# A two-layer convolution-attention hybrid on one Trainium2 core: the order of the first loads, the place of the feed-forward weights, and the first table load

## The chip, the cores and the metric

The kernel runs on one core of a Trainium2 chip. The metric is the device time of one execution in microseconds (us); lower is better. The engines are TensorE (PE, with its weight loads shown apart as PEld), VectorE (DVE), ScalarE (ACT), GpSimd (POOL) and SyncE (SP), which only issues DMAs here. ScalarE and GpSimd can issue DMAs too.

## What is computed

The input x has 4 images of 128 channels and 64 x 64 positions, so each image is a 128 x 4096 matrix. Cut to what matters:

```python
# layer 0, for each image (C = 128 channels, 4096 positions)
xn = group_norm(x)                                  # 32 groups of 4 channels
e1, e2 = prelu(w1 @ xn + b1), prelu(w2 @ xn + b2)   # 64 channels each
asm = prelu(wa @ xn + ba)                           # 128 channels
x = x + softmax(e1.T @ e2, axis=2) @ asm            # 4096 x 4096 scores
# layer 1, on tokens t = x.T (4096 tokens of 128 features)
h = layer_norm(t)
q = products_of_cosines(h + rx_theta)               # 16 heads of 8
a = softmax(q @ q.T / sqrt(8)) @ q                  # q is query, key and value
x1 = layer_norm(h + a @ w_comb.T + b_comb) * g1 + beta1
zf = cos(x1[..., :8]) * cos(ry_theta)
t = t + layer_norm(x1 + relu(zf @ w1.T + b1) @ w2.T + b2) * g2 + beta2
# a recurrence over the positions, y = sigmoid(norm(W t) + y @ V.T)
t = t + recurrence(layer_norm(t))
```

Attention runs per image over all 4096 tokens in layer 1.

## The kernel before

The images are taken one after the other. For each, `first_stage` runs layer 0 (and, beside it, the feed-forward of the image before), and `second_stage` runs layer 1's attention. `last_stage` does the last image's feed-forward, and the recurrence over all images ends the kernel. The order of instructions on TensorE, ScalarE and VectorE is written out by hand within the stages; each engine works its list in order. DMAs and SyncE's list are placed by a scheduler, which also inserts the waits, among them the waits for memory: each stage has pools of tiles, a new stage's tiles lie where earlier tiles lay, and an instruction that writes such a tile waits for the last user of what lay there.

**The start** (lines 135 to 331). GpSimd's queue issues the loads of the first convolutions' weights and biases (`w12_sb`, `b12_sb`, `wa_sb`, `aa_sb`, `a12_sb`), then clears small tiles and builds the group matrix `grp` with two `affine_select`. ScalarE's queue issues 26 loads (line 184 on): `rx_bc`, `wc_sb`, two copies of four bias rows into `biases`, the feed-forward's matrices and rows, and four copies each of `f1T` and `ry`. SyncE issues x in four pieces of 128 x 1024 (`load_x`, line 1513), the third and fourth only when the first and second have landed.

VectorE, once x arrives, takes eight statistics (`gst`, line 350), and between them small preparations: it negates slopes and biases (lines 167 to 169), and turns the bias rows `ba`, `b_comb` and `fb2 + be1` into pairs of a rounded part and a rest in `bias_rows` (lines 324 to 330). `gmv` (line 353), two tiny matmuls with `grp` (lines 357 and 366) and GpSimd's power (line 241) give the mean `gm` and the scale `r_g`. Then come the feed-forward's first weights (lines 312 to 322): `cos_steps` brings `ry` into range on VectorE and ScalarE takes its sine (`cry`), `f1_all` is multiplied by it, split into `f1_sb` and `f1_low`, and a DMA from SyncE puts part of `f1_low` into `f1_sb`. The tiles of this preparation lie in a pool `setup`, closed at line 331; the image's tile `q` may lie on that memory afterwards.

**Layer 0** (`layer0`, line 369). `normalised` writes the normalised image into `q` (line 378), the convolutions follow (lines 391 and 427), `halves` splits e1 into a high and a low part (`hl`), and the loop at line 545 runs over 8 blocks of 512 positions with 32 tiles of scores each, two pairs of tiles a turn: `scores` (line 503, then `exp` at line 507), `weigh` (line 514, with the row sums on VectorE at lines 525 and 528). After each pair the loop calls `meanwhile`, which advances other work by a step: `calls[0]` counts these calls, 16 in a block. From the 18th call, `tokens` (line 606) does a finished block's transposition, sums, layer norm, cosines (table switch and sine at line 255) and products, and stores high and low parts in `parts_dram` (line 699).

**Attention** (`attention`, line 701) loads `queries` and `keys` from `parts_dram` (lines 762 and 771), has GpSimd clear and fill `q_aug` and `mirror` (lines 731 to 748 and 802), and then works through score tiles: line 1057 (scores), 1069 (exponential), 866 and 845 (the two products), 832 (transposition on VectorE).

Of the kernel before, what the change touches and what calls it, by code (L numbers as in the profile page):

```python
# [26 lines left out]
def kernel(  # L27
# [109 lines left out]
    def load(ap, name, shape=None):  # L137
        t = const.tile(list(shape or ap.shape), F32, tag=name, name=name)
        loader[0].dma_start(out=t, in_=ap)
        return t  # L140

    def load_row(ap, name):
        return load(ap.partition_broadcast(P), name, (P, ap.shape[-1]))
# [29 lines left out]
    for sign, base in ((1, 0), (-1, 3)):  # L173
# [7 lines left out]
            channel_multiplier=sign,  # L181
        )
    grp = grp.rearrange("p a b -> p (a b)")
    loader[0] = nc.scalar
    rx_bc = load_row(rx, "rx_bc")
    wc_sb = load(w_combT, "wc_sb")

    f1_sb = const.tile([P, NF, P], F32, tag="f1_sb", name="f1_sb")
    ry_sb = once.tile([P, 1], F32, tag="ry_sb", name="ry_sb")
    nc.gpsimd.memset(ry_sb, 0.0)  # L190
    setup = ctx.enter_context(ExitStack())
    setup_pool = setup.enter_context(tc.tile_pool(name="setup", bufs=1, reuse_waits="tile"))
    f1_all, f1_low = (
        setup_pool.tile([P, NF * P], F32, tag=name, name=name) for name in ("f1_all", "f1_low")
    )
    biases = setup_pool.tile([33, 4, P], F32, tag="biases", name="biases")
    nc.gpsimd.memset(f1_all, 0.0)
    for i in range(2):
        for k, ap in enumerate((ba, b_comb, fb2, be1)):
            nc.scalar.dma_start(out=biases[ds(32 * i, 1), k, :], in_=ap)  # L200
    for g in range(4):
        nc.scalar.dma_start(out=f1_all[ds(D * g, D), :], in_=f1T)
        nc.scalar.dma_start(out=ry_sb[ds(D * g, D), :], in_=ry)
    fb1_sb, f2_sb = load(fb1, "fb1_sb"), load(f2T, "f2_sb")
    g1_bc, be1_z = load_row(g1, "g1_bc"), const.tile([P, D], F32, tag="be1_z", name="be1_z")
    be1_bc = setup_pool.tile([P, P], F32, tag="be1_bc", name="be1_bc")
    nc.scalar.dma_start(out=be1_bc, in_=be1.partition_broadcast(P))
    g2_bc, be2_bc = load_row(g2, "g2_bc"), load_row(be2, "be2_bc")
    WT_sb, VT_sb = load(WT, "WT_sb"), load(VT, "VT_sb")
    gamma_sb, beta_sb = load(gamma, "gamma_sb"), load(beta, "beta_sb")  # L210


    nc.vector.tensor_copy(be1_z, be1_bc[:, 0:D])
    ident = const.tile([P, P], F32, tag="ident", name="ident")
    make_identity(nc, ident)
    ones = const.tile([P, P], F32, tag="ones", name="ones")
# [27 lines left out]
    def cos_steps(dst, arg, k, r):  # L244

        nc.vector.tensor_scalar(k, arg, 1.0 / (2 * math.pi), ROUND, ALU.mult, ALU.add)
        nc.vector.tensor_scalar(k, k, ROUND, None, ALU.subtract)
        nc.vector.scalar_tensor_tensor(r, k, -TWO_PI_1, arg, ALU.mult, ALU.add)
        yield
        nc.vector.scalar_tensor_tensor(r, k, -TWO_PI_2, r, ALU.mult, ALU.add)  # L250
        nc.vector.scalar_tensor_tensor(r, k, -TWO_PI_3, r, ALU.mult, ALU.add)
        yield
        nc.vector.scalar_tensor_tensor(r, r, -1.0, r, ALU.mult, ALU.max)
        yield
        nc.scalar.activation(dst, r, AF.Sin, bias=half_pi[: dst.shape[0]], scale=-1.0)
# [53 lines left out]
        return bc.unsqueeze(1).broadcast_to([P, TG, P])  # L309


    ck = once.tile([P, 1], F32, tag="ck", name="ck")
    cr = once.tile([P, 1], F32, tag="cr", name="cr")
    cry = once.tile([P, 1], F32, tag="cry", name="cry")
    for _ in cos_steps(cry, ry_sb, ck, cr):
        pass
    nc.vector.tensor_scalar(f1_all, f1_all, cry, None, ALU.mult)
    f1_high = f1_sb.rearrange("p f e -> p (f e)")
    nc.vector.tensor_copy(f1_high.bitcast(F32R), f1_all)
    nc.vector.tensor_tensor(f1_low, f1_all, f1_high, ALU.subtract)  # L320

    nc.sync.dma_start(out=f1_high[ds(2 * D, 2 * D), :], in_=f1_low[ds(2 * D, 2 * D), :])

    for row in (0, 32):
        at = slice(row, row + 1)
        nc.vector.tensor_tensor(biases[at, 2], biases[at, 2], biases[at, 3], ALU.add)
        nc.vector.tensor_copy(bias_rows[at].bitcast(F32R), biases[at, 0:3])
    nc.vector.tensor_tensor(
        bias_rows[at].bitcast(F32R), biases[at, 0:3], bias_rows[at], ALU.subtract
    )  # L330
    setup.close()


    def prelu(dst, src, plus, minus, bias, minus_slope):

# [1238 lines left out]
    def first_stage(im, before):  # L1574


        n = im["n"]


        ffn = dict(x1=(HALF, 3), fhalf=(HALF, 7), hT=(MID, 2))  # L1580
        held_late = dict(thalf=(HALF, 6), half=(HALF, 2), hl=(MID, 2))
        rest = dict(e=(BIG, 2), big=(BIG, 1), mid=(MID, 7), sums=(MID, 2))
        pools = {**ffn, **held_late, **rest}
        psum = dict(ps_acc=(ONE, 1), ps_pair=(MID, 2), ps_one=(ONE, 3))
        engines = {nc.tensor.engine, nc.scalar.engine, nc.vector.engine}
        others = {name: one_psum for name in ("ps_norm", "ps_tok")}
        with stage(f"conv{n}", {}, others, **pools, **psum), tc.manual_schedule(engines=engines):
            own, calls = [], [0]
            step_late = in_steps(feed_forwards(before) if before else [], 13, 3)

            def meanwhile(steps=1):

                calls[0] += 1
                if before and calls[0] in (14, 17, 20):
                    before["left"].pop(0)()
                for _ in range(steps):
                    step_first(own)

                for _ in range(0 if calls[0] <= 8 else 2 if calls[0] % 8 == 0 else 1):
                    step_late()  # L1600

            norm = im["norm"] or list(norm_stats(n, im["xs"]))[-1]
            layer0(
                n,
                im["xs"],
                im["q"],
                norm,
                n == "r",
                lambda ic, sums: own.append(tokens(im, ic, sums)),
                meanwhile,  # L1610
            )
            *own, tail = own
            for g in own:
                for _ in g:
                    pass
            while step_late():
                pass
            while not next(tail):
                pass
        return tail  # L1620
# [119 lines left out]
    t2_rows = [t2_dram[ts(n, P), :] for n in range(N)]  # L1740
    before = None
    x_next = {"xs": load_x(0, ts(0, P))}

    def prepare_image(n):

# [5 lines left out]

    for n in range(N):
        image = open_image(n, ts(n, P), "right" if n % 2 else "left", **x_next)
        tail = first_stage(image, before)
        if before:
            before["close"]()
        upcoming = prepare_image(n + 1) if n + 1 < N else iter(())
        second_stage(image, tail, upcoming)
        before = image
# [246 lines left out]
```

## Time and profile before

| what | us |
|---|---|
| median of 3 runs | 6988.64 |
| lowest and highest | 6988.06, 6990.65 |
| profiled execution, device time | 6989.88 |
| its span, first to last instruction | 6988.2 |
| mean granted TensorE clock in it | 0.989 |
| image 0, first normalisation starts | 24.34 |
| image 0, one block of layer 0 | 44.0 |
| image 0, first attention scores | 405.1 |

The profile is of one execution. Its page gives each engine's busy time over the span, and the views used below list instructions in order of time. A line of such a list has the start, the duration, the engine, the source line, the operation with what it writes and reads, and in brackets how long the engine had been idle and which work ended the idle time. "SPq" and "ACTq" are an engine's sequencer issuing a DMA; the bytes travel afterwards. Buffer numbers are left out of names, so `f_sb` is `f1_sb`, `minus_b` is `minus_b12`, `s` and `p` are any of the score and exponential tiles.

### The profile page before, as it was taken

The page shows a single profiled execution, that of the slowest core. Times are in us where ns is not written, and L with a number is a line of the kernel's source. Part 1 is how long each engine was busy: PE and PEld are TensorE (multiplying, and loading weights), DVE is VectorE, ACT ScalarE, POOL GpSimd, SP SyncE. Part 2 cuts the span into 40 slices and gives each one's busy share as a digit, 9 for nine tenths or more (in the row PEclk, how much of TensorE's full clock was granted, in tenths as well). Part 3 has the DMA queues.
Part 4 walks back from the last instruction along what each step waited for, and adds up shares of the span by engine and source line. Part 5 has one row for each costly group of instructions (what it writes and reads, how often), then busy time and mean ns, then how long its engine had stood idle before and what let it go on. Part 6 is the DMA issues. An engine that isn't in the chain of part 4 may idle for free. (4 is left out here: it accounts for less than half of the span.)

```text
span 6988.2 us, 223483 instructions
## 1 busy us (share of the span) xinstructions
PE 6812.8 (97%) x92333; PEld 3660.6 (52%) x92333; DVE 5967.8 (85%) x8064; ACT 5932.7 (85%) x11843; POOL 2786.7 (40%) x10008
## 2 busy tenths in 40 slices
PE   8999999999999999999999999999999999999996
PEld 4545555555664555555565455555466555555554
DVE  6688889987888999888787888888978888898987
ACT  4479999996669999999566999999956699999984
POOL 1134444434333444443433344444343434344442
PEclk9999999999999999999999999999999999999998
DMA  1110000000111000000111100000001100000012
GB/s 32 37 41 25 24 28 21 22 10 23 49 50 42 26 21 22 21 22 9 33 50 49 37 22 21 22 20 24 22 26 47 56 25 22 22 24 29 13 62 109
DMA packets 84760, 219.87 MB, mean 31 GB/s; under 512 B 9384, under 2 KB 10288, under 8 KB 82960
## 3 DMA queue, kind: packets, MB, share of 16 engines
q1 hardware_dynamic: 80448, 200.34, 8.4%
q8 instruction: 726, 11.89, 0.7%
q10 hardware_dynamic: 3024, 4.99, 0.2%
q14 instruction: 306, 2.51, 0.1%
q0 software_dynamic: 256, 0.13, 0.0%
HBM read 141.44 MB, written 56.62 MB: 28 GB/s over the span
## 5 line engine op out<-in xcount | busy, mean ns | idle before, releaser
L1069 ACT ACTIVATE e<-s 128x1024 f32<-128x1024 f32 (+1 forms) x3480 | 2950.0, 901 | 114.8 <-PE s L1057 83.0
L832 DVE STREAM_TRANSPOSE t<-e 128x1024 f32<-128x1024 f32 x2240 | 2594.2, 1210 | 77.3 <-ACT e L1069 74.6
L845 PEld LDWEIGHTS misc<-t,mirror 128*32 128x32 f32 x57344 | 1656.6, 110 | 1327.2 <-issue 1270.8
L845 PE MATMUL misc<-t,mirror 128*32 128x128 f32 x57344 | 1968.3, 273 | 18.6 <-DVE later L859 15.8
L1069 ACT ACTIVATE xs<-s 128x1024 f32<-128x1024 f32 (+1 forms) x2152 | 1838.9, 908 | 55.2 <-PE s L1057 43.0
L832 DVE STREAM_TRANSPOSE t<-xs 128x1024 f32<-128x1024 f32 x1344 | 1562.5, 1210 | 42.7 <-ACT xs L1069 41.2
L866 PE MATMUL acc<-e,q_aug 128*32 128x512 f32 x11360 | 1524.7, 609 | 1.0 <-POOL q_aug L748 1.0
L1057 PE MATMUL s<-queries,keys 32*128 32x512 f32 x9216 | 1243.2, 497 | 20.7 <-ACT e L1069 10.4
L912 POOL COPY own<-o 32x36 f32<-32x36 f32 x2048 | 430.7, 210 | 1807.1 <-DVE o L904 1727.1
L514 PE MATMUL acc<-p,asmT 128*128 128x512 f32 x2048 | 946.2, 593 | 1.8 <-DVE e L410 1.6
L866 PE MATMUL acc<-xs,q_aug 128*32 128x512 f32 x7072 | 942.4, 605 | 0.0
L507 ACT ACTIVATE p<-s 128x1024 f32<-128x1024 f32 x512 | 499.8, 1022 | 403.8 <-PE s L503 399.8
L1057 PEld LDWEIGHTS s<-queries,keys 32*128 32x128 f32 x9216 | 487.2, 182 | 601.4 <-issue 296.2
L937 POOL COPY other<-turned 32x64 f32<-32x64 f32 x1904 | 449.7, 236 | 624.3 <-DVE turned L927 545.8
L1069 ACT ACTIVATION_READ_ACCUMULATOR e<-s 128x1 f32 x2880 | 694.5, 241 | 0.0
L802 POOL COPY mirror<-q 32x128 f32<-32x128 f32 x2048 | 599.3, 293 | 199.2 <-PE misc L845 111.3
L503 PE MATMUL s<-hl,e 128*128 128x512 f32 x2048 | 586.4, 428 | 22.4 <-ACT p L507 10.9
L528 DVE TENSOR_TENSOR total<-total,p 128x1024 f32<-128x1024 f32 x448 | 547.8, 1223 | 22.0 <-ACT p L507 14.3
L514 PEld LDWEIGHTS acc<-p,asmT 128*128 128x128 f32 x2048 | 380.0, 190 | 334.8 <-issue 309.8
L503 PEld LDWEIGHTS s<-hl,e 128*128 128x128 f32 x2048 | 379.9, 189 | 178.3 <-issue 68.6
L1069 ACT ACTIVATION_READ_ACCUMULATOR xs<-s 128x1 f32 x1728 | 421.4, 244 | 0.0
L898 POOL COPY by_token<-by_key 32x4 f32<-32x4 f32 x2000 | 383.8, 192 | 84.4
(314 smaller groups left out, 4459.2 us busy)
## 6 DMA issues: line engine op xcount, KB each, us to landing
keys<-parts_dram SPq DMA_DIRECT2D x256, 256.0 KB
queries<-parts_dram SPq DMA_DIRECT2D x1024, 32.0 KB
x_dram<-x SPq DMA_DIRECT2D x56, 256.0 KB
fx<-x_dram SPq DMA_DIRECT2D x48, 256.0 KB
xs<-in_x_dram SPq DMA_DIRECT2D x16, 512.0 KB
t_dram<-t2T SPq DMA_DIRECT2D x32, 256.0 KB
t2s<-t_dram SPq DMA_DIRECT2D x16, 512.0 KB
hl<-hl SPq DMA_DIRECT2D x28, 256.0 KB
```

Source lines behind the costliest of these rows:

```text
L503: nc.tensor.matmul(s[:, j, :], stationary, moving, start=y == 0, stop=y == len(parts) - 1)
L507: nc.scalar.activation(p, s, AF.Exp)
L514: nc.tensor.matmul(state["acc", ic], asmT[:, ts(2 * jp + j, P)], p[:, j, :], start=jp == 0 and j == 0, stop=jp == NP - 1 and j == 1,)
L528: nc.vector.tensor_tensor(state[ic], state[ic], p, ALU.add)
L802: nc.gpsimd.tensor_copy(wv[ts(a, 32), s, :, :, ts(a, D)], own[ts(s, 32)])
L832: nc.vector.transpose(group["e"][h][:, k, :], es[h])
L845: nc.tensor.matmul(state["acc"][ts(2 * x + h, 32), :], state["w"][:, QT * (s // 4) + TG * x + s % 4, h, :], state["e"][h][:, :, ds(IC * x ...
L866: nc.tensor.matmul(it["in"]["acc"][ts(2 * h + x, 32), :], it["qa"][:, ds((2 * it["tiles"][x] + h) * V, 32)], it["e"][h][:, ts(x, IC)], sta ...
L912: nc.gpsimd.tensor_copy(own[ts(s, 32), ts(x, 4), h, :], ov[ts(2 * h + x, 32), s, :, 0:V])
L937: copy(to[ts(k, 32), h], tv[ts(2 * x + h, 32), k])
L1057: nc.tensor.matmul(ss[h][:, x, :], keys[unit[x] // QT].bitcast(F32R)[r, ts(unit[x] % QT, P)], queries[b].bitcast(F32R)[r, :], start=True, ...
L1069: nc.scalar.activation(es[h][:, ts(x, IC)] if split else es[h], ss[h][:, x, :] if split else ss[h].rearrange("p x c -> p (x c)"), AF.Exp, ...
```

## The change

The loads of x are issued first, by SyncE. Behind them SyncE issues the loads that ScalarE's queue issued before. Of the bias rows only `ba`, which layer 0 needs, is prepared at the start, by a new function `bias_of_third` that borrows the last columns of `q` as room. The rest of the preparation becomes a generator `other_weights`, which takes its room from the pool of feed-forward tiles (`fhalf`, unused in image 0) and is advanced in the calls 6, 26, 29 and 32 of `meanwhile` in image 0. A one-column exponential at the start makes ScalarE load exp's table. The pool `setup` is gone, and so the addresses of other tiles change.

The removed lines at the start, in short, are the loads on ScalarE's queue and the preparation named above (old lines 184 to 213 and 312 to 331). The added ones:

```diff
+    def bias_of_third(room):
+        for row in (0, 32):
+            nc.scalar.dma_start(out=room[row : row + 1, :], in_=ba)
+        for row in (0, 32):
+            at = slice(row, row + 1)
+            nc.vector.tensor_copy(bias_rows[at, 0].bitcast(F32R), room[at, :])
+        nc.vector.tensor_tensor(
+            bias_rows[at, 0].bitcast(F32R), room[at, :], bias_rows[at, 0], ALU.subtract
+        )
+
+    def other_weights():
+        f1_all, f1_low, rows, row = (
+            get("fhalf", name) for name in ("f1_all", "f1_low", "bias_parts", "be1_row")
+        )
+        biases = rows[0:33].rearrange("p (k e) -> p k e", e=P)
+        be1_bc = row[:, 0:P]
+        nc.gpsimd.memset(f1_all, 0.0)
+        nc.gpsimd.memset(ry_sb, 0.0)
+        for i in range(2):
+            for k, ap in enumerate((b_comb, fb2, be1)):
+                nc.sync.dma_start(out=biases[ds(32 * i, 1), k, :], in_=ap)
+        for g in range(4):
+            nc.sync.dma_start(out=f1_all[ds(D * g, D), :], in_=f1T)
+            nc.sync.dma_start(out=ry_sb[ds(D * g, D), :], in_=ry)
+        nc.sync.dma_start(out=be1_bc, in_=be1.partition_broadcast(P))
+        yield
+        nc.vector.tensor_copy(be1_z, be1_bc[:, 0:D])
+        cr, cry = (once.tile([P, 1], F32, tag=name, name=name) for name in ("cr", "cry"))
+        for _ in cos_steps(cry, ry_sb, ck, cr):
+            pass
+        yield
+        nc.vector.tensor_scalar(f1_all, f1_all, cry, None, ALU.mult)
+        f1_high = f1_sb.rearrange("p f e -> p (f e)")
+        nc.vector.tensor_copy(f1_high.bitcast(F32R), f1_all)
+        nc.vector.tensor_tensor(f1_low, f1_all, f1_high, ALU.subtract)
+        yield
+        nc.sync.dma_start(out=f1_high[ds(2 * D, 2 * D), :], in_=f1_low[ds(2 * D, 2 * D), :])
+        for row in (0, 32):
+            at = slice(row, row + 1)
+            nc.vector.tensor_tensor(biases[at, 1], biases[at, 1], biases[at, 2], ALU.add)
+            nc.vector.tensor_copy(bias_rows[at, 1:3].bitcast(F32R), biases[at, 0:2])
+        nc.vector.tensor_tensor(
+            bias_rows[at, 1:3].bitcast(F32R), biases[at, 0:2], bias_rows[at, 1:3], ALU.subtract
+        )
...
-            own, calls = [], [0]
+            own, calls, weights = [], [0], other_weights()
...
                 calls[0] += 1
+                if n == 0 and calls[0] in (6, 26, 29, 32):
+                    next(weights, None)
...
     x_next = {"xs": load_x(0, ts(0, P))}
+    loader[0] = nc.sync
+    rx_bc = load_row(rx, "rx_bc")
+    wc_sb = load(w_combT, "wc_sb")
+    f1_sb = const.tile([P, NF, P], F32, tag="f1_sb", name="f1_sb")
+    ry_sb, ck = (once.tile([P, 1], F32, tag=name, name=name) for name in ("ry_sb", "ck"))
+    be1_z = const.tile([P, D], F32, tag="be1_z", name="be1_z")
+    fb1_sb, f2_sb = load(fb1, "fb1_sb"), load(f2T, "f2_sb")
+    g1_bc, g2_bc, be2_bc = load_row(g1, "g1_bc"), load_row(g2, "g2_bc"), load_row(be2, "be2_bc")
+    WT_sb, VT_sb = load(WT, "WT_sb"), load(VT, "VT_sb")
+    gamma_sb, beta_sb = load(gamma, "gamma_sb"), load(beta, "beta_sb")
...
         image = open_image(n, ts(n, P), "right" if n % 2 else "left", **x_next)
+        if n == 0:
+            bias_of_third(image["q"][:, S - P : S])
+            nc.scalar.activation(ck, half_pi, AF.Exp)
         tail = first_stage(image, before)
```

In layer 0's list on ScalarE this puts a sine table load, the sine `cry` and an exp table load between the exponentials of score tiles 9 and 10 of block 1 (blocks and tiles counted from 0).

More of the change, by code (lines that the diff above doesn't have):

```diff
@@ L183 @@
     grp = grp.rearrange("p a b -> p (a b)")
[L184 to L213, printed above, removed]
     ident = const.tile([P, P], F32, tag="ident", name="ident")
@@ L309, in row4 @@
         return bc.unsqueeze(1).broadcast_to([P, TG, P])
[L312 to L331, printed above, removed]
+    def bias_of_third(room):
[7 more added lines that the diff above has]
+        )
```

## The prediction

> **What bounds the kernel now.** I read the page first, then busy time by stretch, then the first 45 us in order of time, then the place where layer 0 hands over to attention.
>
> ```profile
> span 6988.2 us, 223483 instructions
> PE 6812.8 (97%) x92333; PEld 3660.6 (52%) x92333; DVE 5967.8 (85%) x8064; ACT 5932.7 (85%) x11843; POOL 2786.7 (40%) x10008
> ```
>
> TensorE is busy 97% of the span, so work saved on another engine counts only where TensorE stands still for it. Busy time by stretch (columns: stretch, length, busy time and instructions of PE, PEld, DVE, ACT and POOL, granted clock, DMA share, GB/s) shows where that is:
>
> ```profile
> 0.00:25.00 25.00, 1.20 (x5) 1.05 (x5) 11.80 (x37) 1.58 (x2) 7.78 (x21) 1.00 0.37 122
> 110.00:154.00 44.00, 44.00 (x150) 25.40 (x149) 30.83 (x53) 20.66 (x22) 5.53 (x8) 1.00 0.10 30
> 405.00:450.00 45.00, 37.56 (x488) 16.05 (x486) 43.54 (x64) 39.95 (x83) 25.08 (x75) 0.89 0.07 21
> ```
>
> In the first 25 us TensorE does almost nothing. One block of layer 0 lasts 44 us, all of it TensorE's, while VectorE has 13.2 us and ScalarE 23.3 us to spare. In the first 45 us of attention VectorE is the full engine (43.54 of 45). The change touches all three. The start, in order of time (start, duration, engine, line, operation; in brackets the idle time before and its releaser):
>
> ```profile
> 5.69 0.69 DVE L350 BATCH_NORM_STATS2 gst<-xs 128x6 f32<-128x512 f32 x1 [4.41 <-DMA xs<-in_x_dram]
> ...
> 8.40 0.15 DVE L169 TENSOR_SCALAR minus_b<-b_sb 128x1 f32<-128x1 f32 x1 [2.01 <-DMA b_sb<-in_b_dram]
> 8.47 0.68 DVE L350 BATCH_NORM_STATS2 gst<-xs 128x6 f32<-128x512 f32 x1
> ...
> 12.63 0.28 DVE L326 TENSOR_TENSOR biases<-biases 1x128 f32<-1x128 f32 x1 [1.09 <-DMA biases<-in_be_dram]
> ...
> 16.12 0.37 DVE L353 BATCH_NORM_AGGREGATE gmv<-gst 128x2 f32<-128x48 f32 x1
> ...
> 18.76 0.58 POOL L241 TENSOR_TENSOR r_g<-v_g,minus_half 128x1 f32<-128x1 f32 x1 [10.38 <-DVE v_g L239]
> ...
> 24.34 1.00 DVE L378 TENSOR_SCALAR q<-xs,gm,r_g 128x512 f32<-128x512 f32 x2 [2.16 <-DMA f_sb<-f_low]
> ...
> 24.95 3.78 PE L391 MATMUL pc<-q,w_sb 128*128 128x512 f32 x4 [6.47 <-DVE q L378]
> ...
> 34.92 1.28 ACT L507 ACT_TABLE_LOAD   x1
> ...
> 36.21 1.94 ACT L507 ACTIVATE p<-s 128x1024 f32<-128x1024 f32 x2
> ...
> 37.29 1.98 PE L514 MATMUL acc<-p,asmT 128*128 128x512 f32 x4 [1.55 <-DVE e L410]
> ```
>
> Two things are to be seen. The norm's scale r_g is ready at 19.34 (18.76 + 0.58), but the first normalisation starts at 24.34, because it waits for the copy of f_low (prepared on VectorE in between) to leave the memory that q is given. And the first exponential starts the moment a 1.28 us table load ends, with TensorE waiting behind it. The handover at 405 us:
>
> ```profile
> 396.96 0.60 POOL L731 MEMSET q_aug<- 128x599 f32 x1 [15.06 <-PE s L503]
> ...
> 403.83 1.80 POOL L736 MEMSET mirror<- 128x2048 f32 x1 [6.27 <-PE acc L514]
> ...
> 405.58 5.02 POOL L748 COPY q_aug<-q 32x112 f32<-32x112 f32 x16
> ...
> 410.66 1.94 PE L866 MATMUL acc<-e,q_aug 128*32 128x512 f32 x8 [1.05 <-POOL q_aug L748]
> ```
>
> GpSimd's preparation hangs on TensorE's last layer 0 work, and TensorE then waits 1.05 us for it.
>
> **What the Trainium skill says.** "ScalarE: Activation LUTs", section "What ACT_TABLE_LOAD costs", gives about 1283 ns for a load and about 1380 ns of drain per switch. The load's row agrees (1.28); no drain is visible here, since the activation before ended at 34.90. I price 1.28. The same page, "Table sets: the hidden batching unit", puts exp and the cheap functions in one set; this trace agrees, since the Relus after the sine at 20.12 need no load. "DMA: Bandwidth & Descriptors", section "Issuing engines are not separate DMA queues", says that DMAs of all issuers interleave on the same 16 engines. So GpSimd's first loads will share them with a denser x; the 2 us wait at 8.40 for b_sb is where that would show.
>
> **The change part by part.**
>
> *x first, fewer small loads in front.* Now the third and fourth quarter of x are issued only at 5.68, after the first has landed; in the changed program four go out in a row (two took 0.87 us to issue). VectorE's list still puts minus_b behind the first statistic, so the restart at 8.40 stays if b_sb lands as now. From 8.47 to the end of gmv at 16.49 it loses: the 1.09 wait for the bias row, two additions of bias rows (0.26, 0.28), the copy to be_z (0.17), and about 0.4 because three casts and a subtraction work on 128 elements instead of 384 (0.33, 0.35 and 0.55 now). That is 2.2, less about 0.1 of issue, so 2.1. Against it, b_sb may land later under two more quarters of x. The latest case is behind all of x: 2.1 MB at the 321 to 324 GB/s of the stretches 4 to 6 and 8 to 12 us is 6.5 us from about 2.5, plus a microsecond to signal, so 10.5 instead of 8.4, which eats the whole 2.1. I take 0.8 of delay, nearer to now, because the DMA was almost idle (123 GB/s from 6 to 8 us) when b_sb landed and so was not held by bytes. Gain 1.3, bounds 0 and 2.2.
>
> *Feed-forward weights out of the start.* Between r_g and q stand cos_steps (18.97 to 20.41), three operations of 512 (20.51 to 22.18) and a DMA issued at 22.21 that releases q at 24.34. All go. q can start 0.05 after r_g: 24.34 - 19.39 = 4.95. This has one answer as long as nothing else is late at r_g; w_sb and wa_sb, on GpSimd's queue, landed 6.2 and 4.8 us after issue, before 10.
>
> *Exp's table at once.* The load moves to about 1.7 us, behind two DMA issues on an idle ScalarE. At 34.92 the first scores must be ready: their last three matmuls start at 33.84, and elsewhere in this loop the exponential follows 1.20 to 1.23 us after four such matmuls start (47.03 to 48.23, 49.31 to 50.54), hence 34.9 or a little earlier for three. So all 1.28 is gained: acc may start at 36.01, its asmT is ready at 35.69. What is late next is VectorE's e at 43.18, which had 2.13 us of idle before it. Bounds 0.6 and 1.3.
>
> *The same work inside block 1.* Its arrival costs ScalarE a sine load, 0.29 and an exp load (2.86 together), with the wait for six small VectorE operations in front of the sine. Queued behind it are exponentials 10 and 11, and behind those TensorE's scores 12 two steps later. From the trace of that place: exponential 9 ended at 114.38, the next began at 117.64, an idle 3.26 which holds the sine load, and the exp load, tied to the scores, adds 1.28 to the next. TensorE needs its result only at 121.38. The existing sine of block 1 (124.86 to 129.50) does exactly this and TensorE stays at 44.00 of 44. VectorE gets 1.3 + 1.6 + 1.5 us (8 small ones, three of 512, five on bias rows), against 13.2 spare, 3.92 of it in one piece at 123 to 126.9. SyncE issues 25 more loads, some 0.3 to 0.6 us each, before hl at 66.97; they end near 20 to 25 us. GpSimd's two memsets move behind ident, on an idle engine. Cost 0; if the cover were gone, at most the 2.86 plus 2 of waiting.
>
> *What memory placement drags along.* In the changed program the 24 loads of queries for pair 0 no longer stand behind GpSimd's last read of the tiles under them. They go out four at a time after each block's parts (SyncE issues 0.6 each, 2.4 us in the 11.4 us between 182.4 and 193.75). The keys and hl keep their turn. In the trace TensorE passes from layer 0 to attention at 405 with no wait for queries, so this alone gains nothing. Also q_aug no longer waits for TensorE and mirror waits only for the last scores (396.96), not for the last acc (403.83): q_aug's copies end near 404 instead of 410.6, and the 1.05 goes. Since VectorE is the full engine there, I count only its own wait for GpSimd behind those copies, 0.38 at 418.10, so 0.4; bounds 0 and 1.4. TensorE's order is unchanged throughout, and images 1 to 3 keep their lists.
>
> Sum: 1.3 + 4.95 + 1.28 + 0.4 = 7.9. The profiled execution took 6989.88 around its span of 6988.2; the median shown is 6988.64, 1.2 less. 7.9 off each gives 6982.0 for that execution and **6980.7** for the median, 0.11% less. A measurement of this kernel can tell about 0.2% from no change, 14 us.
>
> **The rivals.**
> *A, the start is freer than thought:* b_sb lands as now and TensorE's 1.05 passes on: 2.2 + 4.95 + 1.28 + 1.4 = 9.8, so 6978.8. For it: b_sb's early landing. Against: VectorE's 43.54 of 45.
> *B, GpSimd's loads queue behind x:* 0 + 4.95 + 0.6 + 0.4 = 5.95, so 6982.7; with aa and a12 late by two more, 6984.7. For it: the 2.01 wait exists already.
> *C, block 1 pays for the work:* 7.9 - 4.9 = 3.0, so 6985.6. For it: two table switches within one block. Against: 44.00 of 44 beside the existing one.
> *D, slower:* the granted clock. It falls to about half in handovers (0.50 from 409 to 415) and over the span of 6988.2 its mean is 0.989, some 77 us of clock lost. A shifted start and changed gaps at 405 could make these falls longer. From 10% more (7.9) the gain is gone; 30% more costs 23 us, so 7003.7. Against: three runs lie within 2.6 us.
> *E, the change does not free q:* if q's memory still waited for a copy, only 1.3 + 1.28 stay, 6986.1. Against: in the changed list q waits for r_g alone.
>
> **How the numbers follow.** Chances: forecast 0.48, A 0.20, B 0.13, C 0.06, E 0.03, D 0.06, and 0.04 for a larger gain that no view shows. The range for 8 in 10 holds the forecast with its unknown costs, A and B: 6976.5 to 6985.0. Within 0.2% lies all but that larger gain, part of A and D's far end: faster by over 0.2% 0.07, within 0.2% 0.88, slower 0.05.
>
> **What would show it.** In the changed profile: q L378 first near 18 with GpSimd's r_g as releaser; the end of gmv near 15.2 (16.5 for B, 14.4 for A); no table load before the first p, which starts about 6.3 us + 1.28 earlier, near 28.7; TensorE at 44 of 44 in the block that holds cry; q_aug's copies ending before attention's first scores. A time under 6975 or over 6986 would prove the working wrong, the first by a gain in attention that I have counted as VectorE's, the second by a stall in block 1 or by the clock.

## The result, and the profile after

| what | before | after |
|---|---|---|
| median, us | 6988.57 (20 runs) | 6978.98 (20 runs) |
| lowest and highest | 6984.30, 6990.65 | 6974.60, 6983.46 |
| ratio, 95% interval | | 0.9986 (0.998 to 0.9993) |
| profiled execution, its span | 6989.88, 6988.2 | 6978.35, 6976.6 |

The change takes 9.6 us off the median, 0.14%. The gain is small, but it is not noise: the whole 95% interval of the ratio lies under 1. The forecast was 6980.7, 7.9 us less than before. Single executions of either kernel scatter by some 2 us (standard deviation), so a step of one microsecond is read from the marks in the profile, that is, from the times at which named instructions start, and not from the times of whole executions.

The page of the changed kernel, its span and its busy times:

```profile
span 6976.6 us, 223479 instructions
PE 6811.8 (98%) x92333; PEld 3655.3 (52%) x92333; DVE 5966.0 (86%) x8067; ACT 5933.7 (85%) x11845; POOL 2788.3 (40%) x10008
```

TensorE's work is the same (6811.8 against 6812.8). Time has gone where TensorE stood still. Busy time by stretch, for the start, for the block of layer 0 that now holds the sine `cry`, and for the first 45 us of attention:

```profile
0.00:25.00 25.00, 7.30 (x25) 4.96 (x26) 9.36 (x27) 3.82 (x6) 7.73 (x21) 1.00 0.37 121
102.50:146.50 44.00, 44.00 (x150) 25.39 (x149) 34.67 (x68) 23.52 (x25) 5.56 (x8) 1.00 0.11 34
398.00:443.00 45.00, 39.73 (x500) 17.77 (x498) 42.11 (x64) 40.68 (x84) 21.09 (x61) 0.85 0.06 19
```

TensorE has 7.30 us of work in the first 25 us instead of 1.20, and it is still busy for 44.00 of 44 in the block that took over the preparation. The start in order of time:

```profile
1.66 1.28 ACT L1768 ACT_TABLE_LOAD   x1 [1.66 <-PEq L2006]
...
4.35 0.69 DVE L350 BATCH_NORM_STATS2 gst<-xs 128x6 f32<-128x512 f32 x1 [3.08 <-DMA xs<-in_x_dram]
...
9.62 0.15 DVE L169 TENSOR_SCALAR minus_b<-b_sb 128x1 f32<-128x1 f32 x1 [4.58 <-DMA b_sb<-in_b_dram]
...
14.99 0.37 DVE L353 BATCH_NORM_AGGREGATE gmv<-gst 128x2 f32<-128x48 f32 x1
...
17.63 0.58 POOL L211 TENSOR_TENSOR r_g<-v_g,minus_half 128x1 f32<-128x1 f32 x1 [9.34 <-DVE v_g L209]
18.24 1.00 DVE L378 TENSOR_SCALAR q<-xs,gm,r_g 128x512 f32<-128x512 f32 x2 [0.70 <-POOL r_g L211]
...
18.84 3.78 PE L391 MATMUL pc<-q,w_sb 128*128 128x512 f32 x4 [1.49 <-DVE q L378]
...
28.74 1.95 ACT L507 ACTIVATE p<-s 128x1024 f32<-128x1024 f32 x2
...
29.82 1.98 PE L514 MATMUL acc<-p,asmT 128*128 128x512 f32 x4 [0.19 <-ACT p L507]
```

Three differences stand out. x comes earlier (4.35, was 5.69), but VectorE then idles 4.58 us for `b_sb` instead of 2.01, so `gmv` ends only 1.13 earlier (15.36, was 16.49). The first normalisation is released by `r_g` itself at 18.24, 6.10 earlier than before. And no table load stands ahead of the first exponential at 28.74, 7.47 earlier than before. That lead is kept through layer 0: matched matmul by matmul, the changed kernel is still 7.5 us ahead when before reaches 382 us. The sine in block 1, on ScalarE:

```profile
104.94 1.94 ACT L507 ACTIVATE p<-s 128x1024 f32<-128x1024 f32 x2 [3.39 <-PE s L503]
...
106.90 1.28 ACT L225 ACT_TABLE_LOAD   x1
...
108.43 0.29 ACT L225 ACTIVATE cry<-cr,half_pi 128x1 f32<-128x1 f32 x1 [0.25 <-DVE cr L223]
...
110.18 1.28 ACT L507 ACT_TABLE_LOAD   x1 [1.46 <-PE s L503]
111.48 1.94 ACT L507 ACTIVATE p<-s 128x1024 f32<-128x1024 f32 x2
```

Both loads and the sine lie in time in which ScalarE would have waited for TensorE's scores anyway; even behind the sine it waits 1.46 us for them. The handover to attention:

```profile
374.34 0.60 POOL L731 MEMSET q_aug<- 128x599 f32 x1
...
391.14 1.80 POOL L736 MEMSET mirror<- 128x2048 f32 x1 [16.21 <-PE s L503]
392.90 6.27 POOL L748 COPY q_aug<-q 32x112 f32<-32x112 f32 x16
...
397.78 0.60 PE L261 MATMUL px<-ident,xs 128*128 128x128 f32 x4
...
403.86 1.93 PE L866 MATMUL acc<-e,q_aug 128*32 128x512 f32 x8
```

GpSimd's copies now end at 399.17, well ahead of TensorE's first product with `q_aug`, whose wait of 1.05 us is gone. The line of `px`, TensorE's first work after layer 0's last products, serves as a mark below; in before it is

```profile
403.60 0.60 PE L291 MATMUL px<-ident,xs 128*128 128x128 f32 x4
```

### The profile page after: what moved, and what is told of

Read it like the earlier page. It is cut to its first block, busy times and chain, and to the rows that moved or that the text cites. A ratio compares the mean times of both kernels' runs of the same rounds, so it can differ in the third digit from the quotient of the medians.

```text
span 6976.6 us, 223479 instructions
## 1 busy us (share of the span) xinstructions
PE 6811.8 (98%) x92333; PEld 3655.3 (52%) x92333; DVE 5966.0 (86%) x8067; ACT 5933.7 (85%) x11845; POOL 2788.3 (40%) x10008
## 5 line engine op out<-in xcount | busy, mean ns | idle before, releaser
L866 PE MATMUL acc<-e,q_aug 128*32 128x512 f32 x11360 | 1523.1, 608 | 0.0
L1057 PE MATMUL s<-queries,keys 32*128 32x512 f32 x9216 | 1243.7, 497 | 20.8 <-ACT e L1069 10.8
L866 PE MATMUL acc<-xs,q_aug 128*32 128x512 f32 x7072 | 942.3, 605 | 0.0
L503 PE MATMUL s<-hl,e 128*128 128x512 f32 x2048 | 588.1, 428 | 21.9 <-ACT p L507 10.8
```

The lines of the kernel that those rows point to most:

```text
L503: nc.tensor.matmul(s[:, j, :], stationary, moving, start=y == 0, stop=y == len(parts) - 1)
L866: nc.tensor.matmul(it["in"]["acc"][ts(2 * h + x, 32), :], it["qa"][:, ds((2 * it["tiles"][x] + h) * V, 32)], it["e"][h][:, ts(x, IC)], sta ...
L1057: nc.tensor.matmul(ss[h][:, x, :], keys[unit[x] // QT].bitcast(F32R)[r, ts(unit[x] % QT, P)], queries[b].bitcast(F32R)[r, :], start=True, ...
```

## Does the profile after repeat itself?

The changed kernel was profiled a second time.

> The changed kernel again, unaltered, for what of its own profile recurs. If the gain is made in the start and kept, all marks of the start recur: first statistic near 4.35 us, minus_b near 9.6, q near 18.2, p near 28.7, and the span is again 8 to 12 us under that of before. Theory 'free clock windows': the four slow adds at 375 us (3.57 us for four) and the last 5 us of difference that appear after 6750 us do not recur in the same size. Rival 'the change makes them': both recur within 0.3 us. Time near 6979, ratio to before near 0.9986.

Measured: 6979.14 us (21 runs), ratio 0.9987 (0.9981 to 0.9994), and the marks of the start are within 0.1 us of the first profile's (`minus_b` 9.65, q 18.26, p 28.77). What did not recur is this. At 374.7 TensorE has waited 3.21 us for a tile of tokens, in both profiles. Its work after that wait, in the first profile of the changed kernel:

```profile
374.68 0.68 PE L261 MATMUL pq<-ident,q 128*128 128x128 f32 x4 [3.21 <-DVE q L681]
375.16 3.57 PE L514 MATMUL acc<-p,asmT 128*128 128x512 f32 x4
```

and in the second:

```profile
374.80 0.63 PE L261 MATMUL pq<-ident,q 128*128 128x128 f32 x4 [3.21 <-DVE q L681]
375.27 1.88 PE L514 MATMUL acc<-p,asmT 128*128 128x512 f32 x4
```

The same four matmuls take 3.57 or 1.88 us. Busy time by stretch shows why, in the first profile

```profile
375.00:380.00 5.00, 5.00 (x14) 2.69 (x13) 4.85 (x5) 0.84 (x2) 0.00 (x0) 0.66 0.39 105
```

and in the second

```profile
375.00:380.00 5.00, 5.00 (x19) 3.10 (x18) 4.93 (x5) 2.41 (x3) 0.06 (x1) 1.00 0.39 103
```

TensorE is "busy" for all of it in both, but at a granted clock of 0.66 it gets through 14 matmuls and at 1.00 through 19. The lead over before shrinks from 7.5 to 5.8 us there in the first profile and stays at 7.4 in the second.

The Trainium skill, "TensorE: Matmul & The Clock Gate", section "What's actually happening", says that the clock is halved after at least one idle window of about 3.4 us, and that these windows run freely, whatever the kernel does. The trace agrees with the free windows: within a profile the records of the clock change only in steps of 3.41 us, so they give the grid of the windows. In the first profile the wait (371.47 to 374.68) takes 2.97 us of the window that ends at 375.12, and the half clock is granted from 375.12 on. In the second (371.59 to 374.80) a window ends at 373.23 in the middle of the wait, no window holds more than 1.64 us of it, and the clock stays full.

All thirteen profiles follow this, those of the variants below among them. Each has a wait of 3.1 to 3.2 us at this place, before too (3.16 us). In the eight with the half clock, one window holds 2.2 to 3.2 us of the wait; in the five without, none holds more than 2.0. The page speaks of an idle window; here 2.2 us of 3.41 were enough. So the half clock at this place is the luck of how the grid lies in an execution. Seven of the eight profiles with the preparation in the loop show it, and one of the five without; as before has the same wait, nothing here shows that the change makes it.

Of the last 5 us of difference, the part after 6896 us recurred (2.8 and 2.7 us); the 2.3 us that the first profile gained between 6781 and 6896 did not. So the theory holds for the clock and for that stretch, and something steady is left at the very end (below).

## Which part of the change brings what

**The order of the loads alone.** The kernel before, with x first and all of ScalarE's loads behind it on SyncE; the preparation stays in the start.

```diff
-    loader[0] = nc.scalar
+    x_rows = x.rearrange("n c s -> (n c) s")
+    xs_first = by_channel.tile([P, S], F32, tag="xs", name="xs0")
+    for i in range(4):
+        nc.sync.dma_start(out=xs_first[:, ts(i, S // 4)], in_=x_rows[ts(0, P), ts(i, S // 4)])
+    loader[0] = nc.sync
...
-        nc.scalar.dma_start(out=f1_all[ds(D * g, D), :], in_=f1T)
+        nc.sync.dma_start(out=f1_all[ds(D * g, D), :], in_=f1T)
```

> The kernel before with x's four loads first and every other load behind them on SyncE; the feed-forward weights are still prepared in the start, with the sine there. Theory (the 6.1 us at q come from taking the preparation out of the start, x first is worth about 1 us at gmv alone): gmv ends 1 to 2 us earlier than the 16.49 of before, q is not released before 23.5 us (it waits for the weights' copy, whose inputs come later than before), p near 35.5 to 37, time within 1.5 us of before. Rival (x first is what matters): q near 18 to 20, p near 30, time near 6981.

In order of time, of this variant:

```profile
14.14 0.37 DVE L357 BATCH_NORM_AGGREGATE gmv<-gst 128x2 f32<-128x48 f32 x1
...
21.24 0.65 SPq L326 DMA_DIRECT2D f_sb<-f_low  x1
23.38 1.00 DVE L382 TENSOR_SCALAR q<-xs,gm,r_g 128x512 f32<-128x512 f32 x2 [2.16 <-DMA f_sb<-f_low]
...
33.96 1.28 ACT L511 ACT_TABLE_LOAD   x1
```

`gmv` ends 1.98 us earlier than before (14.51), yet q gains only 0.96, since it still waits for the weights' copy. (The expectation's bounds of 23.5 and 35.5 were missed by 0.12 and 0.25: p is at 35.25.) The time is 6985.49, ratio 0.9997 (0.9988 to 1.0005), so by the ratio x first alone can't be told from before. But the median is 3.0 us below that of the runs of before beside it (6988.45), which misses the expected 1.5, and the means are 2.6 apart (1.5 to 3.8, with single executions taken as independent, as in all comparisons of means here). That is more than the 0.96 at q. The rest fits a pause at the very end that is missing in this variant too (below).

**The preparation alone.** The changed kernel with the weights' loads put back on ScalarE's queue, ahead of x.

```diff
+    loader[0] = nc.scalar
+    rx_bc = load_row(rx, "rx_bc")
+    wc_sb = load(w_combT, "wc_sb")
...
     x_next = {"xs": load_x(0, ts(0, P))}
-    loader[0] = nc.sync
-    rx_bc = load_row(rx, "rx_bc")
-    wc_sb = load(w_combT, "wc_sb")
...
```

> The changed kernel with the weights' loads back on ScalarE's queue ahead of x; the preparation stays in the loop and the early exponential stays. Theory (taking the preparation out is the main part): gmv ends as in before, near 16.5 us (15.36 in the changed kernel), q near 19.3, p near 29.9, so 1.1 us of the 7.5 are lost and the time is near 6980. Rival (the order of the loads is the main part): q not before 22 us, p not before 33, time near 6984.

In order of time:

```profile
16.70 0.37 DVE L363 BATCH_NORM_AGGREGATE gmv<-gst 128x2 f32<-128x48 f32 x1
...
19.96 1.00 DVE L388 TENSOR_SCALAR q<-xs,gm,r_g 128x512 f32<-128x512 f32 x2 [0.70 <-POOL r_g L221]
...
30.28 1.95 ACT L517 ACTIVATE p<-s 128x1024 f32<-128x1024 f32 x2
```

p comes 5.93 us earlier than before without the order of the loads, and 7.47 with it. So the preparation is the main part, and the order is worth 1.5 us once nothing else holds q. (`gmv`, q and p came 0.6, 0.7 and 0.4 us later than expected; `gmv` ends at 17.07, against 16.49 in before, as `minus_b` comes at 8.97 and a statistic waits for x at 13.04. A part of the 1.5 is therefore lost by this variant rather than gained by the order.) The time was 6981.43, ratio 0.9986 (0.998 to 0.9993), against 6990.84 for the runs of before beside it. The same runs of before, 2.3 us slower than those of the result, also stand beside the next two variants, whose times are to be read against them. Its mean is 1.8 us (0.6 to 3.1) above that of the run with the eight sines, which has the loads in the changed order; that fits the 1.5. Above the run without the exponential it is 2.6 (0.8 to 4.4).

**The early exponential.** The changed kernel without that one line.

```diff
-            nc.scalar.activation(ck, half_pi, AF.Exp)
```

> The changed kernel without its early one-column exponential. Theory (the 1.28 us at p come from having no sine in the start, not from that line): a table load still comes ahead of the first ScalarE operation of the start, p has none before it, p starts near 28.7 us as in the changed kernel, time as the changed kernel's, 6979. Rival (the line brings the 1.28 us, as the prediction has it): a table load stands directly before p, p near 30.0 us, time 1.3 us above the changed kernel.

In order of time, ScalarE's only table load before the loop, and its first exponential:

```profile
9.96 1.28 ACT L398 ACT_TABLE_LOAD   x1 [9.96 <-DMA b_sb<-in_b_dram]
...
29.09 1.95 ACT L507 ACTIVATE p<-s 128x1024 f32<-128x1024 f32 x2
```

The line isn't needed. A table load comes before ScalarE's first Relu (L398) in any case, and the exponential runs on what it loaded: none stands before p. p is 0.35 later than in the changed kernel, which is `b_sb` landing 0.34 later in this one profile (`minus_b` at 9.96, 9.62 there). So the 1.28 us come from taking the sine out of the start, which made ScalarE load a table twice. The time was 6980.50, ratio 0.9984 (0.9977 to 0.9991), 10.3 us below the before beside it: nothing is lost without the line.

**The cover in the loop.** The changed kernel with eight one-column sines more, whose results nobody uses (they ran between 136.6 and 196.4 us).

```diff
+            SINES = (36, 38, 40, 42, 52, 54, 56, 58)
...
+                if n == 0 and calls[0] in SINES:
+                    nc.scalar.activation(again, half_pi, AF.Sin)
```

> The changed kernel with eight added one-column sines, four each in blocks 2 and 3 of the first layer 0 loop, each of which makes ScalarE load the sine's table and then the exponential's. Theory (ScalarE has room there, so the switch for the prepared weights cost nothing): TensorE's chain in these blocks stays dense, the marks at the end of the loop (near 394 us) are within 0.5 us of the changed kernel's and the time is unchanged. Rival C (the loop pays for a switch): up to 2.9 us each, 23 us in all, visible as waits of TensorE on ScalarE in blocks 2 and 3.

Busy time of two stretches of a block's length, in this variant:

```profile
146.50:190.50 44.00, 44.00 (x149) 25.40 (x148) 30.81 (x53) 31.70 (x35) 5.50 (x8) 1.00 0.11 33
190.50:234.50 44.00, 44.00 (x149) 25.40 (x148) 30.81 (x53) 25.73 (x28) 5.48 (x8) 1.00 0.12 34
```

ScalarE works 11 and 5 us more than its 20.66 of the changed kernel in either stretch, TensorE still 44.00 of 44. After the loop the marks are within 0.05 us of the changed kernel's, and the time is 6979.85, 11.0 below the before beside it (the changed kernel: 9.6 and 9.3 below its own). Switches as dense as those with sine loads at 179.36, 185.24, 190.01 and 194.91 us, each with an exponential's load after it, are free there. So rival C, the loop that pays for the work, has no support.

**The handover.** Does the wait for `q_aug` hang on where tiles lie in memory? The kernel before, with one tile of the feed-forward's pool used in image 0, so that other tiles lie elsewhere:

```diff
+            if n == 0:
+                nc.gpsimd.memset(get("fhalf", "pad")[:, 0:1], 0.0)
```

> The kernel before with one added one-column memset of a fhalf tile in image 0, which changes where the tiles of the attention of image 0 lie and nothing else. Theory (the handover's stall in before is a matter of where tiles lie): the start is as before (q 24.3 us, p 36.2), the copies of q_aug no longer hold the add L866 (its wait of 1.05 us goes), and the time is 0 to 1 us below before. Rival (the stall hangs on the attention's own order): the wait of 1.05 us stays.

In order of time:

```profile
383.60 0.60 POOL L731 MEMSET q_aug<- 128x599 f32 x1
...
405.40 0.60 PE L291 MATMUL px<-ident,xs 128*128 128x128 f32 x4
...
411.47 1.94 PE L866 MATMUL acc<-e,q_aug 128*32 128x512 f32 x8
```

The memset no longer waits for TensorE, and from `px` to the product L866 it takes 6.07 us instead of 7.06 (and 6.08 in the changed kernel). So 1.0 us of the change at this place comes from memory placement alone. (Placement also lets the loads of `queries` out early, in this variant as in the changed kernel; since the wait of before was one for `q_aug`, the microsecond is put down to that tile, but no run separates the two.) It can't be seen in the time (6986.75, ratio 0.9999, 0.9991 to 1.0007): in this profile layer 0 had begun with

```profile
35.69 1.94 ACT L507 ACTIVATE p<-s 128x1024 f32<-128x1024 f32 x2
...
36.76 3.78 PE L514 MATMUL acc<-p,asmT 128*128 128x512 f32 x4 [1.19 <-DVE e L410]
```

that is, at half clock (1.98 us in before), although p was 0.52 earlier than there; block 1 was then 1.77 us later than before. Matched matmul by matmul, 0.7 us of the microsecond is left at 450 us, and 0.85 in both profiles of the changed kernel. Whether that reaches the end of attention stays open: the marks at 1767 us differ between profiles by more than that, as half-clock stretches come and go.

## A gain that nobody had expected, at the very end

From the writing of the flag `bad_int`, the last computation, to the end of the span it takes 14.1 us in before and 11.55 in the changed kernel. The trace's records of SyncE's last semaphore steps (us after `bad_int`, semaphore waited for):

```
before   9.63 S[114]   9.71 S[115]  12.45 S[103]  12.54 S[104]  12.60 S[105]
after    9.79 S[116]   9.86 S[117]   9.93 S[103]   9.99 S[104]  10.06 S[105]
```

SyncE stands still for 2.7 us between two steps. In the padded kernel the pause (2.5 us) lies two steps later, before S[105], and SyncE has two instructions fewer there (2097 recorded, 2099 in before). That speaks against a wait for a semaphore; it suggests a fixed place in SyncE's own stream of instructions. To test it, 16 loads of a few bytes that nothing reads were added to before, on SyncE:

```diff
+                if n == 0 and calls[0] in range(36, 52):
+                    k = calls[0] - 36
+                    nc.sync.dma_start(out=again[0:D, k : k + 1], in_=ry)
```

> The kernel before with 16 added loads of a few bytes that SyncE issues during blocks 2 to 4 of the first loop, where its queue is idle; nothing reads what they bring. In the profiles of before and of the padded kernel SyncE stands still for 2.7 and 2.5 us between two of its last semaphore steps after the flag bad_int is written, in the changed kernel and in the other variants (which all issue more on SyncE) it does not. Theory (the pause hangs on where in SyncE's own stream of instructions its last steps fall; SyncE recorded 2099 instructions in before and 2125 in after): with 16 more the pause is gone, from bad_int to the end of the span 11.1 to 11.5 us in place of 14.0, start unchanged (q 24.3, p 36.2), time 2 to 3 us below before, near 6986. Rival (it hangs on ScalarE's loads or on the preparation's place): the pause stays, 13.8 to 14.1 us, time as before.

The pause is gone (11.28 us after `bad_int` in place of 14.1). But the scheduler had put the 16 loads at 10.7 us, ahead of the weights' copy, so q came at 27.39 and p at 39.26, 3.05 later than before; the time was 6989.60, ratio 1.0002 (0.9994 to 1.001). The second try let VectorE set their target in block 2, so that they can't go out earlier:

```diff
+                if n == 0 and calls[0] == 35:
+                    nc.vector.memset(again, 0.0)
```

> As the variant with 16 added small loads on SyncE, but their target is first set by VectorE in block 2, so that they cannot be issued before that (in the first try they stood ahead of the weights' copy and put p at 39.3 us). Theory (the pause among SyncE's last steps hangs on where they fall in its own stream): start as before (q near 24.2, p near 36.0), no pause, from bad_int to the end of the span 11.1 to 11.5 us in place of 14.0, time 2 to 3 us below before, near 6986. Rival: the pause stays, 13.8 to 14.1 us, time as before.

The start is as before (q 24.41, p 35.93), the pause is gone (11.56 us), and the span is 6987.7: layer 0 again began at half clock, and block 1 was 2.0 us late. The time, 6987.48, ratio 0.9997 (0.9989 to 1.0005), leaves it open whether anything changed and misses the expected 6986; the mean is 2.1 us (0.7 to 3.5) below that of before beside it, close to what the pause is worth. By the profiles the rival falls: ScalarE's loads and the preparation's place are as in before, and the pause is gone. In all profiles with 2114 or more instructions on SyncE (eleven) it is absent, in both with fewer it is there. In both cases with the pause an instruction transfer of 16 KB runs within it (9.82 to 10.82 us in before), which fits a late fetch; but such transfers run at about that time in the others too (9.72 to 10.70 in the variant with x first, without a pause), so the cause isn't shown, only that moving the stream removes the pause from this place. If it has a fixed place in SyncE's stream, the 15 or more added instructions move it ahead of the 7.3 us in which SyncE waits for the last transfers anyway, where it would cost nothing; no run tells whether it is still there.

## A version that beats both

The changed kernel's own new wait is the 4.58 us of VectorE for `b_sb`. It is there only because the negations of slopes and biases stand between the first and the second statistic. Moved behind the group means:

```diff
+    def negate():
+        for t in (a12_sb, aa_sb):
+            nc.vector.tensor_scalar(t, t, -1.0, None, ALU.mult)
+        nc.vector.tensor_scalar(minus_b12, b12_sb, -1.0, None, ALU.mult)
...
-            norm = im["norm"] or list(norm_stats(n, im["xs"]))[-1]
+            norm = im["norm"]
+            if not norm:
+                for k, norm in enumerate(norm_stats(n, im["xs"])):
+                    if n == 0 and k == NIC:
+                        next(im["early"], None)
+                    if n == 0 and k == NIC + 1:
+                        negate()
```

(`early` is `bias_of_third`, with a pause after its loads, so that its three operations on VectorE come behind the statistics too.)

> The negations of slopes and biases and the preparation of the attention biases are moved behind the last normalisation matmul, so VectorE's 8 statistics no longer wait for b_sb. Theory (b_sb's arrival at 9.6 sets gmv in the changed kernel): the statistics run from 4.35 us to about 10.3 us, gmv ends near 11 us in place of 15.36, q is released near 14 us in place of 18.24, p near 24.5 in place of 28.74, and the time is 4 to 4.5 us below the changed kernel's, near 6974.5. Rival (x's last two pieces come as late as b_sb): gmv not before 14 us, p not before 27.5, gain under 1.3 us.

In order of time:

```profile
4.39 2.68 DVE L354 BATCH_NORM_STATS2 gst<-xs 128x6 f32<-128x512 f32 x4 [3.12 <-DMA xs<-in_x_dram]
...
7.98 1.29 DVE L354 BATCH_NORM_STATS2 gst<-xs 128x6 f32<-128x512 f32 x2 [0.90 <-DMA xs<-in_x_dram]
...
9.54 1.29 DVE L354 BATCH_NORM_STATS2 gst<-xs 128x6 f32<-128x512 f32 x2 [0.28 <-DMA xs<-in_x_dram]
...
10.86 0.37 DVE L357 BATCH_NORM_AGGREGATE gmv<-gst 128x2 f32<-128x48 f32 x1
...
14.11 1.00 DVE L382 TENSOR_SCALAR q<-xs,gm,r_g 128x512 f32<-128x512 f32 x2 [0.70 <-POOL r_g L214]
...
24.62 1.94 ACT L511 ACTIVATE p<-s 128x1024 f32<-128x1024 f32 x2
```

The statistics now wait for x alone, and p is 4.12 us earlier than in the changed kernel. The time is 6973.47, ratio to before 0.998 (0.9972 to 0.9988), 5.7 us below the changed kernel run beside it (means 5.1 apart, 95% interval 3.4 to 6.7). It is the best of all: 15 us below the runs of before beside it.

What is late next there is the convolution: its four matmuls take 3.78 us, where later ones take 1.88. Matmuls of ones, whose result nobody reads, were put ahead of them to raise the clock:

```diff
+                    if n == 0 and k in (0, NIC + 1, NIC + 2):
+                        spin({0: 12, NIC + 1: 1, NIC + 2: 3}[k])
```

> The variant with the statistics first, with 16 added matmuls of ones on TensorE ahead of the first convolution (12 before the group means, 1 and 3 behind them), whose result nobody reads. Theory (after 14 us of little work TensorE runs its first 4 convolution matmuls at half clock, 3.78 us where later ones take 1.88): they take 1.9 to 2.2 us, p starts 2 to 3 us earlier than the 24.62 of the statistics-first variant, time 1.5 to 3 us below its 6973.5. Rival (the added matmuls hold up the group means, or the clock has dropped again by then): q later than 14.5 us or the four still 3.5 us or more, time the same or worse.

The 12 ended at 6.5 us, the convolution still took 3.78 us, and `gmv` came 0.45 later, since the statistics waited longer for x in that execution. The time is 6976.02, in the mean 12.8 us (11.6 to 14.1) below the runs of before beside it; the statistics-first variant, run at another time, was 14.2 (12.7 to 15.7) below those beside it. With 22 in place of 12:

> The statistics-first variant with 26 added matmuls of ones ahead of the first convolution (22, 1 and 3; the 16 of the first try ended at 6.5 us, 5 us ahead of the group means, and the convolution was at half clock again). Theory: TensorE is kept busy to about 10.9 us, the first four convolution matmuls take 1.9 to 2.2 us in place of 3.78, p near 22 to 23, time 1.5 to 3 us below the statistics-first variant's. Rival (a short spell of little work at the group means is enough to halve the clock): the four take 3.5 us or more, p near 24.6 to 25.2, time no better than the statistics-first variant's.

In order of time:

```profile
1.28 8.15 PE L1614 MATMUL spare<-ones 128*128 128x512 f32 x22 [1.28 <-DVE half_pi L192]
...
14.46 3.56 PE L395 MATMUL pc<-q,w_sb 128*128 128x512 f32 x4 [0.70 <-DVE q L382]
```

The clock did rise (22 matmuls in 8.15 us, where 12 took 5.24; the tiny ones of the group means took 0.35 instead of 0.56). But from 9.4 us to 14.5 TensorE has little to do, the records of the clock show the half clock from 14.25 us, and the convolution is slow again. p is at 24.14, 0.48 earlier than without the filling, and the time is 6977.51, in the mean 12.3 us (10.8 to 14.0) below before. So neither run gained anything, and the theory of both fell; whether the filling loses time isn't settled, as these runs were not taken side by side with the statistics-first variant. A version with denser filling wasn't tried.

## Why the prediction was right

Its verdict (within 0.2% of before) held, and its range, 6976.5 to 6985.0, holds the 6978.98. That a change of under 0.2% can't be told from none was too cautious: this one was told, by runs side by side. Step by step:

| step of the sum | forecast | measured | where |
|---|---|---|---|
| x first, at `gmv` | 1.3 (0 to 2.2) | 1.13 | end of `gmv` 16.49 to 15.36 |
| `b_sb` later by | 0.8 | 1.22 | `minus_b` 8.40 to 9.62 |
| preparation out of the start | 4.95 | 4.97 | q 6.10 earlier, less 1.13 |
| exp's table | 1.28 (0.6 to 1.3) | 1.37 | p 7.47 earlier, less 6.10 |
| the work in block 1 | 0 | 0 | TensorE 44.00 of 44 |
| handover | 0.4 (0 to 1.4) | 1.0 there, 0.85 at 450 us | wait of 1.05 gone |
| pause at the end | not in the sum | 2.6 gain | 14.1 to 11.55 |
| half clock at 375 us | not in the sum | 1.7 loss, by luck of the window | lead 7.5 to 5.8, or kept |

The large steps were read from waits that the trace of before names: q's release by the weights' copy, and the table load directly ahead of p. Removing such a wait was worth the distance to the next releaser, and that came out within 0.1 us. The three steps of the start were forecast at 7.53 us and came to 7.47. The dearer doubt, whether the loop pays for the moved work (rival C), was decided by TensorE's 44.00 of 44, and the eight added sines show how much room there was.

Four things were less right.

- The reason given for the third step was off: it is the missing sine and not the early exponential that frees p. The prediction took the Relus after the sine as a sign that the exponential's table set also holds the Relu; in before they run on what was loaded for the sine, so they show only that this one does. It is the variant without the exponential that shows a load made for a Relu to serve the exponential.
- In the first step two errors partly cancelled: `b_sb` was delayed more than assumed (1.22 us against 0.8), and the work and waits removed were worth 2.35 instead of 2.1. The mechanism of rival B, GpSimd's loads behind x, was nearly all there: x's last packet ended at 9.07 us, `b_sb` landed at 9.52 and `a12_sb` at 11.48 (8.29 and 9.44 in before). It cost little, since by then all of x had come and VectorE took its statistics without a further wait. The latest case for `b_sb` also adds up to 10.0, not 10.5: 2.5, 6.5 and about 1 to signal (0.83 in before, from the last packet of x's first quarter at 4.86 to the first statistic at 5.69).
- At the handover all of TensorE's wait went, where VectorE was taken for the limit, though a part of it was lost again in the next 40 us.
- The pause at the end was in no term of the sum.

The time came 1.7 us under the forecast. The pause (2.6) and the handover's surplus (0.45) are more than that, and a half clock that falls in one execution and not in another takes some of it back. This sum should not be read finely, as the marks of single profiles drift by 2 to 3 us over the later stages. So the nearness of the start is understanding, and that of the whole is in part luck: a gain that no view had shown fell within the range. Of the rivals, A gave the nearest time (6978.8), also by luck, since `b_sb` did land later and the handover gave less than A had. Rival D, the clock, has its mechanism in the runs (half clock at 375 us), but before has the same wait there, and at 1.7 us a time it could not turn the sign.

## What to carry to other kernels

Where the trace names the releaser of the first heavy instruction, look for the next releaser: the distance between the two was the gain here, twice, and it could be read before anything was changed. Work taken out of such a start was free in a loop in which one engine is full (44.00 of 44) and the others wait for it. After moving a load ahead, look at which small load it delays and whether anything long stands behind that one in an engine's list: here the preparation of three columns and one bias row, by operations of 0.14 to 0.3 us, cost 4.1 us.

## What the runs showed of the hardware

- The end of the program has a pause of 2.5 to 2.7 us on SyncE that comes and goes with the number of instructions on SyncE (seen at 2097 and 2099, not from 2114 to 2129), far larger than the instructions themselves. Its cause is not shown.
- The clock was halved after a window of the 3.41 us grid in which one wait left TensorE idle for 2.2 us or more (eight profiles), and not where no window held more than 2.0 us of the wait (five profiles).
- Small loads on GpSimd's queue landed 1.2 us later (`minus_b` 8.40 to 9.62, and 9.63 to 9.96 in four further profiles with x first) when x's four large loads were issued in a row on SyncE and the other loads behind them, though they were issued at the same time, 2.67 us. Which of SyncE's loads delay them is not separated; with ScalarE's loads ahead of x, as in before, but the preparation in the loop, `minus_b` came at 8.97.
- TensorE's clock in the first 25 us is not what the column says: it shows 1.00 where four matmuls took 3.78 us, twice as long as later. Before the first record of the clock, the durations are the better witness.
